# Where the residual's statistics, the weight checks and the token splits stand in a transformer block on one core

## The chip, the core and the metric

The kernel runs on one core of a Trainium2 chip. The core has five engines, each with an instruction queue of its own that runs in order: TensorE (PE in the profile, with its weight loads as PEld), VectorE (DVE), ScalarE (ACT), GpSimd (POOL) and SyncE (SP), which here issues nearly all DMAs. The metric is the device time of one execution in microseconds, as the median of three runs.

## The reference, cut to what matters

One transformer block on two sequences of 1024 tokens of 1024 numbers. Six vectors per sequence (shift, scale and gate, for attention and for the FFN) come from a conditioning vector. Then:

```python
h   = layernorm(x) * (1 + scale_a) + shift_a
q, k, v = split(clip(h @ Wqkv.T, -8, 8));  q, k = layer_norm(q), layer_norm(k)
p   = softmax(q @ k.T * 32**-0.5 + alibi, causal)          # 32 heads of 32
x1  = x + gate_a * ((p @ v) @ Wout.T)                      # the residual
h2  = layernorm(x1) * (1 + scale_f) + shift_f
g   = (h2 @ Wg.T) * ag;  u = (h2 @ Wu.T) * au              # Wg, Wu: 2752 x 1024
out = x1 + gate_f * (((silu(g) * u) @ Wd.T) * ad)
```

All data are float32. The FFN weights hold only -1, 0 and 1.

## The kernel before, in words

**Products.** Each large product is cut into two by two blocks and done with seven block products instead of eight (`SEVEN`, L780): P1, P2, U2, P5, U3, P53, U6 in this order, each a chain of matmuls into one of two PSUM banks, x and y in turn, so that a chain can begin when the bank's previous result has been read. `seven` (L843) runs such a group of chains: after every few matmuls it yields and calls `between`, and after each chain `read` evicts the bank. The sums of blocks that the scheme needs of its operands (S1 to S4, T1 to T4) are made on VectorE and GpSimd. Matmuls are recorded on L748, transposes on L751.

**Stages.** From 0 to about 580 us: modulation and the QKV projections. Then attention, with the dense work of the projections and of `output` dealt into its gaps by a planner (`together`). `output(b, js)` is the out-projection: for each sequence b it goes over pairs j of token tiles (a pair is 2 x 128 rows, four pairs a sequence). All pairs of sequence 0 and pairs 0 and 1 of sequence 1 run inside attention; pairs 2 and 3 of sequence 1 run `alone` after it (from about 1307 us), with `after=first_tokens`, so that the first FFN step is dealt in among the last pair. Then the FFN: `gate_up(b)` goes over eleven steps p of 256 of the 2752 columns, first for b=0, then b=1 (the boundary lies near 1680 us), and at the end the down product.

**One pair of `output`.** `read` copies P1, U2 and P5 on ScalarE (L1357). For P2, U3 and P53 VectorE adds the bank to the copy (L1365), GpSimd multiplies by the gate (L1366) and adds to the rows `xr` of x (L1367). For U6, VectorE multiplies the bank by the gate (L1363) and GpSimd adds it (L1367). Then `normalize` takes the statistics of the two row tiles: four `bn_stats` of 512 columns (L714) and two `bn_aggr` (L715) on VectorE, the moment the pair's chains have been issued. Each L714 waits for its L1367. The remainder is deferred: `todo.first(go)` keeps a function that the next `todo.place()` runs, inside the next pair's chains; it issues the two stores of x1 (L1380, SP) and `rest_` (L719 to L731: VectorE's small operations, ScalarE's L721 and L726, and the normalized rows, L731, over `xr`). Behind it, from chain number q0 = 3 of the next pair on, come four groups of transposes (L751), whose evictions write `h2t` (L871 on VectorE; in the last pairs half on ScalarE, L873), and `token_operands` (L1231 and L1232 on VectorE, L1233 and L1234 on GpSimd, stores to `hs` in memory on SP, L1237). An order without a semaphore between two instructions of one engine is written with `behind(a, b)`; `hold` puts an instruction behind the latest read of a bank in this way.

**One FFN step.** Two chains at a time, g and u, four banks gx, ux, gy, uy. Seven token operands hs_0 to hs_6 (1 MB each) are loaded (L1609, SP) once per sequence and split into a high and a low part: `tokens_split`, a cast on ScalarE (L1614) and a subtraction on VectorE (L1615). The weights of the next step are staged by SP (L1593), and from them `weight_operands` makes three casts on ScalarE (L1692, L1693, L1700) and four sums on GpSimd (S1 L1694, S2 L1697, S3 L1698, S4 L1699). `check_weights` counts weights that are not small integers: for each of two halves a cast to int8 on ScalarE (L1655) and a compare on VectorE (L1656). Evictions are L1808 on ScalarE, L1813 and L1828 on VectorE; silu is L1825; sums of the activations are L1769. The very first S1 has an order behind the last L1367 of sequence 1's pair 2 (`last_sum`), with no semaphore. `in_range` (L1408 to L1411) is a test of the softmax sums, four VectorE operations, issued at the end of attention.

## Time and profile before

| what | value |
|---|---|
| median of 3 runs | 2265.51 us (2263.86 to 2270.93) |
| the profiled execution | 2262.51 us, of it a span of 2260.7 us |
| TensorE busy | 2143.8 us, 95% |
| VectorE, GpSimd, ScalarE busy | 1352.1, 1098.0, 943.3 us |
| granted TensorE clock, mean | 0.984 |

Times in the profile are microseconds from the span's start. A line of a timeline gives start, duration, engine, line, operation, what it writes and reads, how many were run together, and in brackets how long the engine stood idle just before and what ended that. A line of the waits gives the sum of such idle times, their number and the longest. The lines of a table by stretch give the stretch, its length, each engine's busy time with its instructions, the granted clock, the share of the DMA engines and GB/s. Line numbers are those of the kernel before.

### The profile page before, as it was taken

To read this page: it belongs to the slowest core of one execution; us is meant where nothing else is said; L and a number is where in the kernel's file an instruction comes from. 1 tells how busy PE (TensorE), PEld (TensorE's weight loads), DVE (VectorE), ACT (ScalarE), POOL (GpSimd) and SP (SyncE) were. 2 spreads that over 40 slices of the span, in tenths; PEclk is the share of its full clock that TensorE was granted. 3 is DMA by queue.
4 is the path that set the end of the run, shared out by engine and by line. 5 is a ranking of instruction groups with operands and counts; after the bars stand their busy time and mean duration, and the time that the engine had idled before them with its cause. 6 is when DMAs were issued, how large, how long until landed. Compare 5 with 4: busy or idle time off the path is not lost. (4 is left out here: it accounts for less than half of the span.)

```text
span 2260.7 us, 27238 instructions
## 1 busy us (share of the span) xinstructions
PE 2143.8 (95%) x9537; PEld 1170.8 (52%) x9537; DVE 1352.1 (60%) x1811; ACT 943.3 (42%) x1782; POOL 1098.0 (49%) x775
## 2 busy tenths in 40 slices
PE   5999999999999999899999888899998999999998
PEld 2444444333333333232222235788877888788887
DVE  5775653455566633457667676788976555534535
ACT  1222223445444445466555414554554444333331
POOL 2330112443344554586677563677977667312212
PEclk9999999999999999999999999999999999999999
DMA  9877776545425531854553366767758777598765
GB/s 370 321 288 265 293 276 240 184 145 194 168 80 199 174 116 48 281 171 140 148 168 103 100 204 205 216 206 245 251 195 256 242 228 233 202 379 314 275 225 189
DMA packets 319349, 482.44 MB, mean 213 GB/s; under 512 B 16092, under 2 KB 235036, under 8 KB 310244
## 3 DMA queue, kind: packets, MB, share of 16 engines
q1 hardware_dynamic: 316752, 472.19, 62.4%
q10 hardware_dynamic: 2452, 8.43, 1.0%
q8 instruction: 77, 1.26, 0.2%
q14 instruction: 68, 0.56, 0.1%
HBM read 323.01 MB, written 157.55 MB: 213 GB/s over the span
## 5 line engine op out<-in xcount | busy, mean ns | idle before, releaser
L1103 ACT ACTIVATE p<-sc,kw 128x128 f32<-128x128 f32 (+3 forms) x1024 | 422.1, 513 | 390.1 <-PE sc L748 365.5
L748 PE MATMUL bank<-wT,a 128*128 128x512 f32 x768 | 366.6, 611 | 14.1 <-DVE wT L834 7.9
L1135 POOL TENSOR_TENSOR p<-p,p 128x1024 f32<-128x1024 f32 (+3 forms) x128 | 263.4, 2058 | 212.8 <-PE av L748 186.0
L1135 DVE TENSOR_TENSOR p<-p,p 128x1024 f32<-128x1024 f32 (+3 forms) x192 | 242.7, 1281 | 110.8 <-POOL p L1107 68.2
L748 PE MATMUL bank<-wB,a 128*128 128x512 f32 x576 | 270.2, 605 | 1.2 <-DVE raw L993 0.6
L748 PEld LDWEIGHTS bank<-wT,a 128*128 128x128 f32 x768 | 136.8, 191 | 200.2 <-issue 167.1
L1107 POOL TENSOR_SCALAR_AFFINE_SELECT p<-p 128x256 f32<-128x256 f32 x256 | 137.1, 548 | 182.3 <-ACT p L1103 171.3
L748 PE MATMUL sc<-cq,ck 32*128 32x512 f32 (+3 forms) x1536 | 181.6, 538 | 11.7 <-DMA ck<-qk 8.4
L748 PE MATMUL av<-p,cv 128*32 128x512 f32 (+3 forms) x1536 | 168.8, 500 | 13.2 <-POOL p L1107 13.0
L748 PEld LDWEIGHTS bank<-wB,a 128*128 128x128 f32 x576 | 102.1, 189 | 141.9 <-issue 128.8
L1899 DVE TENSOR_TENSOR lo<-lo,hi 128x1408 fp32r<-128x1408 f32 x56 | 96.3, 1723 | 93.1 <-ACT hi L1898 93.1
L748 PEld LDWEIGHTS sc<-cq,ck 32*128 32x128 f32 x1536 | 61.8, 184 | 149.8 <-issue 82.4
L1898 ACT CAST hi<-lo 128x1408 fp32r<-128x1408 f32 x56 | 76.9, 1375 | 134.0 <-DMA lo<-act 89.7
L1963 POOL TENSOR_TENSOR early_P<-early_P,x1in 128x512 f32<-128x512 f32 x16 | 35.7, 2234 | 165.1 <-DVE early_P L1961 160.3
L748 PEld LDWEIGHTS av<-p,cv 128*32 128x32 f32 x1536 | 33.7, 108 | 146.5 <-issue 80.9
L1694 POOL TENSOR_TENSOR wS<-wst,wst 128x1024 fp32r<-128x1024 f32 (+1 forms) x22 | 65.9, 2997 | 87.5 <-PE uy L748 61.9
L993 DVE TENSOR_TENSOR raw<-P,bank 128x512 f32<-128x512 f32 x48 | 32.8, 684 | 119.1 <-PE bank L748 98.9
L748 PE MATMUL gx<-hs,wS 128*128 128x512 f32 (+1 forms) x352 | 90.6, 399 | 10.6 <-ACT gP L1808 7.0
L748 PE MATMUL gy<-hs,wS 128*128 128x512 f32 (+1 forms) x352 | 89.4, 396 | 9.5 <-DVE gP L1813 6.4
L748 PE MATMUL gx<-hs,wA 128*128 128x512 f32 (+1 forms) x352 | 89.0, 393 | 1.5 <-ACT h2t L873 1.5
L748 PE MATMUL uy<-hs,wS 128*128 128x512 f32 (+1 forms) x352 | 87.2, 390 | 1.2 <-DVE uP L1813 1.2
L748 PE MATMUL ux<-hs,wS 128*128 128x512 f32 (+1 forms) x352 | 88.3, 393 | 0.0
(266 smaller groups left out, 3996.3 us busy)
## 6 DMA issues: line engine op xcount, KB each, us to landing
lo<-act SPq DMA_DIRECT2D x56, 704.0 KB
a<-hop SPq DMA_DIRECT2D x20, 1792.0 KB
wm<-in_L_wmod_dram SPq DMA_DIRECT2D x48, 512.0 KB
act<-aS SPq DMA_DIRECT2D x88, 256.0 KB
wB<-in_L_attn_Wqkv_dram SPq DMA_DIRECT2D x21, 1024.0 KB
wst<-in_L_ffn_Wg_dram SPq DMA_DIRECT2D x40, 512.0 KB
wst<-in_L_ffn_Wu_dram SPq DMA_DIRECT2D x40, 512.0 KB
qk<-qs SPq DMA_DIRECT2D x16, 1024.0 KB
```

What stands on the lines that cost most here:

```text
L748: return in_order(nc.tensor.matmul(*args, **kw_))
L993: nc.vector.tensor_add(dst, part_t[MATE[q]], bank)
L1103: last_exp[0] = nc.scalar.activation(p[:, g, lo:hi], sp[:, g, lo:hi], AF.Exp, bias=kw[:, d, h_ : h_ + 1])
L1107: last_mask[0] = nc.gpsimd.affine_select(out=p[:, :, 0:P], in_=p[:, :, 0:P], pattern=[[0, 2], [1, P]], compare_op=ALU.is_ge, fill=0.0, bas ...
L1135: adders[b](half, jb).tensor_add(dst, dst, ps[half][:, :, 0:n])
L1694: ins = nc.gpsimd.tensor_add(f["S1"], raw["A21"], raw["A22"])
L1898: nc.scalar.copy(hi, lo.bitcast(FP))
L1899: nc.vector.tensor_sub(lo, lo.bitcast(FP), hi.bitcast(FP))
L1963: eng.tensor_add(y, y, x1_of.pop(s))
```

## The change

1. `normalize` is split into `stats` and `rest_`. `output` no longer issues the statistics at the end of a pair, but hands `(stats, go)` to `todo.first`; the first `place()` runs `stats`, each `bn_stats` ordered behind the latest eviction (`last_evict`), and the next one runs `go`. For the two pairs that run alone the places begin one chain later (`when=2`), and their transposes at chain 5 instead of 3. After the very last pair both run at once.
2. `last_sum` is now the last normalized row write (L731) of sequence 1's pair 2, and the first S1 waits for it with a semaphore.
3. `in_range` moves from the end of attention to step 2 of the first `gate_up`, held behind the latest bank read.
4. The check of weight pair 1 moves from chains 4 and 5 of step 0 to chains 0 and 1 of step 1; that of pair 0 from the start of step 1 of the second sequence to chains 4 and 5 of its step 0. The token splits of the second sequence move: hs_0, 1, 2 at chains 2, 4, 6 of the last step of the first sequence and hs_3 to hs_6 at chains 0 to 3 of the next step, where there were five and two.

```diff
@@ -682,12 +682,11 @@
 
         tc.keep_in_program_order(nc.scalar.preload_act_table_set("natural_log_exp_and_others"))
 
-    def behind(ins, first):
-
+    def behind(ins, first, sync=False):
+
+        cls = mybir.DependencyClass.Sync if sync else mybir.DependencyClass.NoSync
         tc.add_manual_dep(
-            ins.ins, first.ins.name,
-            mybir.DependencyInfo(mybir.DependencyClass.NoSync, mybir.DependencyReason.DATA),
-            reason="behind",
+            ins.ins, first.ins.name, mybir.DependencyInfo(cls, mybir.DependencyReason.DATA), reason="behind",
         )
 
     last_exp = [None]
@@ -701,18 +700,28 @@
             behind(ins, last_mask[0])
         return ins
 
-    def normalize(tiles, outs, small, nm):
+    last_evict = [None]
+    last_norm = [None]
+
+    def normalize(tiles, outs, small, nm, split=False):
 
 
 
 
         n = len(tiles)
         mv = small.tile([P, n, 2], FP, tag="mv", name=f"mv_{nm}")
-        for m, t in enumerate(tiles):
-            st = small.tile([P, 2, 6], FP, tag=f"st{m}", name=f"st_{nm}_{m}")
-            for j in range(2):
-                nc.vector.bn_stats(st[:, j, :], t[:, ts(j, HALF)])
-            nc.vector.bn_aggr(mv[:, m, :], st)
+
+        def stats():
+            for m, t in enumerate(tiles):
+                st = small.tile([P, 2, 6], FP, tag=f"st{m}", name=f"st_{nm}_{m}")
+                for j in range(2):
+                    ins = nc.vector.bn_stats(st[:, j, :], t[:, ts(j, HALF)])
+                    if split and last_evict[0] is not None:
+                        behind(ins, last_evict[0])
+                nc.vector.bn_aggr(mv[:, m, :], st)
+
+        if not split:
+            stats()
 
         def rest_():
             ve = small.tile([P, n], FP, tag="ve", name=f"ve_{nm}")
@@ -728,9 +737,11 @@
             nc.vector.tensor_mul(ve, ve, rstd)
             nc.vector.scalar_tensor_tensor(rstd, ve, 1.5, rstd, ALU.add, ALU.mult)
             for m, (t, o) in enumerate(zip(tiles, outs)):
-                nc.vector.tensor_scalar(o, t, mv[:, m, 0:1], rstd[:, m : m + 1], ALU.subtract, ALU.mult)
-
-        return rest_
+                ins = nc.vector.tensor_scalar(o, t, mv[:, m, 0:1], rstd[:, m : m + 1], ALU.subtract, ALU.mult)
+            if split:
+                last_norm[0] = ins
+
+        return (stats, rest_) if split else rest_
 
 
 
@@ -868,7 +879,7 @@
         for j in range(4):
             k = 4 * g + j
             if j % 2 == 0 or not shared:
-                nc.vector.tensor_scalar(dst(k), tp[:, j, :], mul(k), add(k), ALU.mult, ALU.add)
+                last_evict[0] = nc.vector.tensor_scalar(dst(k), tp[:, j, :], mul(k), add(k), ALU.mult, ALU.add)
             else:
                 last_act[0] = nc.scalar.activation(
                     dst(k), tp[:, j, :], AF.Identity, scale=mul(k), bias=add(k)
@@ -895,27 +906,32 @@
 
         def place(self):
             if self.due is not None:
-                self.due()
-                self.due = None
+                due, self.due = self.due, None
+                if isinstance(due, tuple):
+                    due[0]()
+                    self.due = due[1:] if len(due) > 2 else due[1]
+                else:
+                    due()
 
         def add(self, go):
             self.list.append(go)
 
         def run(self, n, all_=False):
-            self.place()
+            while self.due is not None:
+                self.place()
             for _ in range(min(n, len(self.list))):
                 if not all_ and (self.banks.reserved or not self.banks.fresh()):
                     return
                 self.list.pop(0)(self.banks.turn())
                 yield TURN
 
-        def places(self, q0, n, side=lambda e: None):
+        def places(self, q0, n, side=lambda e: None, when=1):
 
             order = [q for _, _, _, q in SEVEN]
 
             def between(q):
                 side(order.index(q))
-                if order.index(q) > 0:
+                if order.index(q) >= when:
                     self.place()
                 if order.index(q) >= q0:
                     yield from self.run(n)
@@ -1360,27 +1376,30 @@
 
                 yg = part_t[MATE.get(q, "P5")]
                 if q == "U6":
-                    nc.vector.tensor_mul(yg, ga[:, ts(n, HALF)], bank)
+                    last_evict[0] = nc.vector.tensor_mul(yg, ga[:, ts(n, HALF)], bank)
                 else:
-                    nc.vector.tensor_add(yg, yg, bank)
+                    last_evict[0] = nc.vector.tensor_add(yg, yg, bank)
                     masked(nc.gpsimd.tensor_mul(yg, yg, ga[:, ts(n, HALF)]))
-                ins = masked(nc.gpsimd.tensor_add(xs[m][:, ts(n, HALF)], xs[m][:, ts(n, HALF)], yg))
-                if (b, j) == (B - 1, NJ - 2):
-                    last_sum[0] = ins
-
-            yield from seven(lambda q, i: a[q][:, i, :], bt, banks, read, todo.places(q0, 1, ahead), 2 if after else 1)
+                masked(nc.gpsimd.tensor_add(xs[m][:, ts(n, HALF)], xs[m][:, ts(n, HALF)], yg))
+
+            yield from seven(lambda q, i: a[q][:, i, :], bt, banks, read, todo.places(5 if after else q0, 1, ahead, when=2 if after else 1), 2 if after else 1)
             yield from todo.run(len(todo.list), True)
             if after is not None and j == NJ - 1:
                 after()
             xn = xs
-            rest = normalize(xs, xn, sm, f"f{b}_{j}")
-
-            def go(xs=xs, qts=qts, rest=rest):
+            stats, rest = normalize(xs, xn, sm, f"f{b}_{j}", split=True)
+
+            def go(xs=xs, qts=qts, rest=rest, j=j):
                 for m in range(2):
                     nc.sync.dma_start(x1_dram[b * NT + qts[m]], xs[m])
                 rest()
-
-            todo.first(go, b == 1 and j == NJ - 1)
+                if (b, j) == (B - 1, NJ - 2):
+                    last_sum[0] = last_norm[0]
+
+            todo.first((stats, go), False)
+            if b == 1 and j == NJ - 1:
+                todo.place()
+                todo.place()
             h2 = keep(b, j)
             for m in range(2):
                 for g in range(2):
@@ -1405,8 +1424,8 @@
 
     def in_range():
 
-        nc.vector.tensor_scalar(most, most, RS_MAX, None, ALU.is_le)
-        nc.vector.tensor_scalar(least_r, least_r, RS_MIN, None, ALU.is_ge)
+        hold(nc.vector.tensor_scalar(most, most, RS_MAX, None, ALU.is_le))
+        hold(nc.vector.tensor_scalar(least_r, least_r, RS_MIN, None, ALU.is_ge))
         nc.vector.tensor_mul(most, most, least_r)
         nc.vector.tensor_reduce(fine, most, mybir.AxisListType.X, ALU.min)
 
@@ -1568,7 +1587,6 @@
     beside[0] = False
     att.close()
     opools, _, bt, todo, _ = out_args
-    in_range()
     ff = ctx.enter_context(ExitStack())
     gu = ctx.enter_context(ExitStack())
     ffp = [ff.enter_context(tc.tile_pool(name="ff_a", bufs=1, space=PSUM))]
@@ -1693,7 +1711,7 @@
                 hold(nc.scalar.copy(f["A12"], raw["A12"]), last_copy)
                 ins = nc.gpsimd.tensor_add(f["S1"], raw["A21"], raw["A22"])
                 if (b, p) == (0, 0):
-                    behind(ins, last_sum[0])
+                    behind(ins, last_sum[0], sync=True)
                 nc.gpsimd.tensor_sub(f["S2"], g["S1"], raw["A11"])
                 nc.gpsimd.tensor_sub(f["S3"], raw["A11"], raw["A21"])
                 nc.gpsimd.tensor_sub(f["S4"], raw["A12"], g["S2"])
@@ -1740,15 +1758,16 @@
 
             def gate_up(b):
                 tiles = [hs_tiles[b, i] for i in range(7)]
+                here = None
                 for p in range(NPR):
                     n = PAIRS[p][1]
                     if p == 1:
                         pinned[0] = True
+                    if (b, p) == (0, 2):
+                        in_range()
                     if (b, p) == (0, 0):
                         operands_of[b, p] = weight_operands(p, staged.pop(0), b)
                     W = operands_of.pop((b, p))
-                    if (b, p) == (1, 1):
-                        check_weights(0, first_staged[0])
                     if p + 1 < NPR or b + 1 < B:
                         base[0] = 0 if (b, p) == (0, 0) else 2 - base[0]
                         staged.append(stage((p + 1) % NPR))
@@ -1771,19 +1790,26 @@
                             keep_act(q, act[q])
 
                     for e, (c_, qa, qb_, q) in enumerate(SEVEN):
-                        split = {(0, 0): (0, e + 2), (0, NPR - 1): (1, e - 2), (1, 0): (1, e + 5)}.get((b, p))
-                        if split is not None and 0 <= split[1] < 7:
-                            tokens_split(*split)
+                        split = {
+                            (0, 0): {i: i + 2 for i in range(5)}, (0, NPR - 1): {2: 0, 4: 1, 6: 2},
+                            (1, 0): {i: i + 3 for i in range(4)},
+                        }.get((b, p), {}).get(e)
+                        if split is not None:
+                            tokens_split(b if p == 0 else b + 1, split)
+                        if (b, p) == (0, 1) and e < 2:
+                            check_weights(1, here, (e,))
+                        if (b, p) == (1, 0) and e in (4, 5):
+                            check_weights(0, first_staged[0], (e - 4,))
                         if e == 3 and wdst is not None:
                             down_parts(p_, wdst)
                         if e == 4 and nb < B:
                             here = staged.pop(0)
                             operands_of[nb, np_] = weight_operands(np_, here, nb)
-                            if nb == 0:
+                            if nb == 0 and np_ > 1:
                                 check_weights(np_, here, (0,))
                             elif np_ == 0:
                                 first_staged[0] = here
-                        if e == 5 and nb == 0:
+                        if e == 5 and nb == 0 and np_ > 1:
                             check_weights(np_, here, (1,))
                         if b and p == NPR - 1 and e == 2:
                             for i in range(2):
```

## The prediction, as recorded before the changed kernel ran

> **What bounds the kernel now.** I read the page first, then the list of waits (all engines, then TensorE's own), then TensorE's timeline around each wait that the diff touches, then VectorE's timeline just before it, and last the busy time and clock by stretch. The page:
>
> ```profile
> span 2260.7 us, 27238 instructions
> PE 2143.8 (95%) x9537; PEld 1170.8 (52%) x9537; DVE 1352.1 (60%) x1811; ACT 943.3 (42%) x1782; POOL 1098.0 (49%) x775
> ```
>
> TensorE is the bound: 117 us of the span are all it stands idle, and no other engine passes 60%. A change that moves no matmul can only win back idle time, and the time that TensorE then runs at half clock. So the question is which idle pieces end at an instruction that the change moves.
>
> ```profile
> engine line waited for: us in total, times, longest us
> DVE st_f L714 <- POOL xr L1367: 67.9, 28, 4.8
> ```
>
> ```profile
> PE bank L748 <- DVE oP L1365: 12.0, 3, 6.4
> PE bank L751 <- DVE h2t L871: 11.2, 9, 3.8
> PE gx L748 <- ACT gP L1808: 7.0, 2, 4.6
> PE gy L748 <- DVE gP L1813: 6.4, 1, 6.4
> ```
>
> The first fence (all engines) says that VectorE, whose queue runs in order, stood 67.9 us in front of the statistics L714, because these wait for GpSimd's residual sum L1367. The second (TensorE's waits) shows who was standing behind it: bank evictions L1365 and L871. TensorE's timeline, in three places, with idle time in brackets:
>
> ```profile
> 1087.19 1.12 PE L751 MATMUL bank<-ident,xr 128*128 128x128 f32 x4 [2.21 <-DVE h2t L871]
> ...
> 1232.55 0.65 PE L751 MATMUL bank<-ident,xr 128*128 128x128 f32 x4 [3.80 <-DVE h2t L871]
> ...
> 1325.69 3.68 PE L748 MATMUL bank<-wT_o,aoS 128*128 128x512 f32 x4 [3.26 <-DVE oP L1365]
> ...
> 1360.80 3.78 PE L748 MATMUL bank<-wT_o,aoS 128*128 128x512 f32 x4 [6.36 <-DVE oP L1365]
> ...
> 1455.50 3.65 PE L748 MATMUL gx<-hs,wS 128*128 128x512 f32 x8 [4.63 <-ACT gP L1808]
> ...
> 1728.89 3.52 PE L748 MATMUL gy<-hs,wS 128*128 128x512 f32 x8 [6.42 <-DVE gP L1813]
> ```
>
> VectorE just before three of them:
>
> ```profile
> 1230.54 0.69 DVE L714 BATCH_NORM_STATS2 st_f<-xr 128x6 f32<-128x512 f32 x1 [3.06 <-POOL xr L1367]
> ...
> 1351.44 0.69 DVE L714 BATCH_NORM_STATS2 st_f<-xr 128x6 f32<-128x512 f32 x1 [1.38 <-POOL xr L1367]
> 1353.85 2.31 DVE L727 TENSOR_TENSOR ve_f<-ve_f,rstd_f 128x2 f32<-128x2 f32 x1
> 1358.62 1.53 DVE L731 TENSOR_SCALAR xr<-xr,mv_f,rstd_f 128x1024 f32<-128x1024 f32 x2
> 1360.07 0.68 DVE L1365 TENSOR_TENSOR oP<-oP,bank 128x512 f32<-128x512 f32 x1
> ...
> 1724.89 3.34 DVE L1656 SCALAR_TENSOR_TENSOR junk<-junk,wst 128x2048 int8<-128x2048 int8 x1
> ```
>
> The statistics hold VectorE, the eviction comes behind them, and TensorE waits for its bank. At 1353.85 a 128x2 operation took 2.31 us; at 1322.82 the same line took 0.16. GpSimd's first weight sums (L1694, L1697, L1699, 1351.37 to 1358.57) ran beside the slow one. At 1724.89 a check stands where an eviction is due. Last, the clock (the last-but-two column) by stretch:
>
> ```profile
> 1084.00:1092.00 8.00, 5.79 (x24) 1.74 (x24) 6.84 (x14) 3.02 (x8) 6.90 (x5) 0.79 0.48 114
> 1228.00:1240.00 12.00, 8.20 (x36) 2.56 (x38) 5.88 (x12) 4.46 (x8) 6.87 (x7) 0.86 0.40 112
> 1340.00:1370.00 30.00, 23.64 (x57) 11.03 (x56) 19.11 (x22) 4.97 (x8) 19.25 (x12) 0.83 0.39 124
> 1452.00:1462.00 10.00, 6.50 (x22) 5.31 (x23) 8.83 (x11) 4.76 (x8) 7.12 (x5) 0.83 0.54 170
> 1720.00:1735.00 15.00, 8.58 (x31) 6.61 (x31) 13.48 (x11) 4.77 (x7) 12.27 (x6) 0.77 1.00 315
> ```
>
> After each such wait TensorE gets half clock for a while: 8 x 0.21, 12 x 0.14 and 10 x 0.17 are each 1.7 us lost. The wait at 1360.80 loses 3.0: half clock runs to 1366.7 by the lengths of the matmuls, 5.9 us at half. That at 1325.69 loses 1.7, that at 1728.89 about 1.6 (half clock to 1732.0).
>
> [...]
>
> **The change, part by part.** The sum is made against the profiled execution (span 2260.7, 1.8 us around it, 2262.51 in all), which lies 3.0 under the median of 2265.51. Instructions stay the same in number on every engine but for one more table load on ScalarE.
>
> A. *Statistics a step later, while attention still runs.* Four L714 of 0.69 and two L715 of 0.2 per pair, 3.2 us of VectorE, are as long as before, but stand behind the U6 eviction of their pair or the next chain's first read, and the two stores and the rest one place later. What they waited for is then done. Gone: 2.21 + 3.80 + 0.48 (a small one at 1069.42) idle, 2 x 1.7 clock, 9.9 in all. What is late next is the rest (L719 to L731, about 2.8 us) in front of some later read: the wait at 1060.48 (2.35, L1365 behind L731) stays. The 5.66 us at 1293.36 ends at GpSimd's L1107 and stays. I take 9, bounds 4 (a wait as at 1232.55 with its clock loss, 5.5, comes up in another place) and 10.
>
> B. *The two last pairs, and the first FFN step* (1310 to 1417.9). With the statistics behind the next P2 read, L1365 at 1324.96 and 1360.07 need not wait for them. Gone: 3.26 + 1.7 + 6.36 + 3.0 = 14.3. The first weight sum now waits, by a semaphore, for L731 of pair 2; behind it on GpSimd stand L1697 and L1699 and the last pair's residual sums. By walking the new order with the old durations, L731 ends near 1350, the three sums (7.04 us) near 1357, and TensorE asks for them past 1362: hidden, with about 5 us in hand; without that cover every microsecond is one on TensorE. Pair 3 starts 8 us sooner by the walk (1336 for 1343.98), so the store of x behind which SP holds the loads of hs also goes 8 us sooner. SP now has four hs loads ahead of the h2t stores of pair 2, and x_10, x_11 behind the rb and aoA loads (which no longer wait for L1367 at 1321.28). Transposes come three chains later (q0 3 to 5), squeezed into P53 and U6, the cost of which is already in the rows (0.6 each). The four range operations (3.1 us of VectorE at 1310 to 1315) leave for a place where VectorE has slack. In the first FFN step TensorE waits eight times now, 0.93, 0.99, 1.96, 0.62, 1.60, 0.51, 0.58 and 1.48, 8.7 in all, mostly for splits of hs (L1614, L1615). These don't go with certainty, since TensorE arrives sooner and a load of 1 MB came 5.5 us after its issue (1351.87 to 1357.38). Best: 14.3 plus two thirds of 8.7, 20. Worst: 9 of the 14.3 is handed on to these waits, 5. I take 14, the eviction waits alone.
>
> C. *Checks of weight pair 1, one step later.* Two L1656 (2.28 each, 4.28 and 4.48 beside GpSimd's sums at 1441 and 1448) and two L1655 of 1.9 move from the end of the first step to chains 1 and 2 of the next. The built order puts both in front of the eviction L1813 of uy, whose bank TensorE wants 12.7 us into the step. They wait for ScalarE's copies, and these for hs stores that landed 9.4 us into it: that is a new wait of 0.5 to 5 us. Against it, the weights of the next pair (which landed at 1438.2) and their checks come sooner, and the 4.63 + 1.7 at 1455.50 shrink. I take +2, bounds -5 and 6.
>
> D. *Batch boundary.* Seven splits are dealt 3 and 4 over two steps for 5 and 2, and pair 0's two checks come out of the step where they held L1813 from 1722.68 to 1728.15. Gone there: 6.42 + 1.6. In the first step of the second batch L1614 no longer stands before L1808: 2.35, and some of 1.19 + 0.4 and 1.6 of clock. 13.5 at best; at worst the four splits (2.3 to 3.3 each), with the checks, now overrun that step, where VectorE had 11 us idle, and 2 is left. I take 8.
>
> Sum 9 + 14 + 2 + 8 = 33; 2262.5 - 33 = 2229.5 for an execution like the profiled one, 2232.5 beside the median.
>
> **The rivals.** *Handed on.* TensorE comes to the first FFN step early and stands there for hs: B is 5 and C -3, total 19, 2246.5. For it: eight waits there already, on four engines. Against it: the loads go earlier too, and DMA was at 0.39 from 1340 to 1370.
>
> *Slower: the loads of hs block the evictions.* In the new order ScalarE has L1614 of hs_0 ahead of the last pair's P5 copy, and of hs_2, hs_1 and hs_3 between the h2t evictions; VectorE has L1615 between the same. If hs_0 lands after 1351 by the walk (P5's copy must be out by 1353.4, after a cast of 1.90), TensorE waits for each load in turn. Price: seven times cast and subtraction, 1.90 + 2.28, with 1.7 of clock, 41 us, less the 5.1 that splits cost now, 36 lost, and B not gained: 9 + 8 - 36 = -19, 2284.5. The walk puts the landing at 1349, 2 us before the point.
>
> *Nothing to measure.* The new places are an order only, and all four parts come out at their low ends: 4 + 5 - 5 + 2 = 6, 2259.5. Against it: the built order does move every statistic that TensorE waited for.
>
> **How the numbers follow.** Forecast 0.66 (its own range 2217 to 2243), handed on 0.22, nothing to measure 0.06, slower 0.06. The upper bounds sum to 49, thus 2217 below; above I go to 2258, through the handed-on case with its unknowns. A difference of 0.3%, 6.8 us, is about what a measurement of this kernel can tell from none: faster 0.88, same 0.06, slower 0.06.
>
> **What would show it.** A right: no idle over 1 us before L751 near 1087 and 1233. B right: no wait for L1365 over 1 us after 1310, and the second FFN step begins by 1404 (1417.89 now). C: the waits at the second step's uy and at the third step's gx add up to less than 5. D: no wait for L1813 over 2 us in the second batch. Wrong: the L714 line of the waits still near 68, or TensorE's idle after 1310 moved to gx and gy behind L1614 or L1615.

## The result, and the profile after

| what | before | after |
|---|---|---|
| median, runs side by side | 2264.69 us (4 runs, 2259.39 to 2270.93) | 2235.15 us (4 runs, 2232.28 to 2239.52) |
| the profiled execution | 2262.51 us, span 2260.7 | 2235.17 us, span 2233.4 |
| granted clock, mean | 0.984 | 0.988 |

The ratio is 0.9879, with an interval of 0.9864 to 0.9894: the changed kernel is 1.2% faster, and 2.7 us from the forecast of 2232.5. That nearness is partly luck: profiled execution against profiled execution the gain is 27.3 us for the 33 forecast, and the stages show errors on both sides. I cut both profiled executions at the same instructions: the first matmul on the ones (end of attention), the first gx matmul of FFN step 1 (the second step; they count from 0), the starts of steps 2 and 3, and the two steps at the batch boundary.

| part | stretch | before, us | after, us | gain | forecast (bounds) |
|---|---|---|---|---|---|
| A | start to the ones | 1293.99 | 1288.06 | 5.9 | 9 (4 to 10) |
| B | ones to FFN step 1 | 123.90 | 107.12 | 16.8 | 14 (5 to 20) |
| C | FFN steps 1 and 2 | 25.56 + 31.86 | 32.48 + 32.09 | -7.2 | +2 (-5 to 6) |
| D | boundary, two steps | 31.50 + 33.54 | 27.20 + 25.39 | 12.4 | 8 (2 to 13) |
| | everything else | | | -0.7 | 0 |
| | sum | | | 27.3 | 33 |

Three parts are inside their bounds; C is outside and has the other sign. The page of the changed kernel:

```profile
span 2233.4 us, 27234 instructions
PE 2135.3 (96%) x9537; PEld 1169.8 (52%) x9537; DVE 1339.3 (60%) x1811; ACT 945.7 (42%) x1783; POOL 1100.6 (49%) x775
```

TensorE's matmuls are as many as before and 8.5 us shorter in sum (2143.8 before), at a mean granted clock of 0.988 for 0.984: half clock avoided; TensorE's idle time (the span less its busy time) is down from 117 to 98 us. The waits of all engines, then TensorE's own (sum, times, longest):

```profile
engine line waited for: us in total, times, longest us
DVE st_f L718 <- POOL xr L1383: 5.4, 4, 3.6
```

```profile
PE av L759 <- POOL p L1123: 16.4, 11, 4.8
PE uy L759 <- DVE uP L1839: 5.8, 2, 4.4
PE bank L762 <- DVE h2t L882: 4.4, 7, 1.8
PE gy L759 <- DVE gP L1839: 3.7, 1, 3.7
PE bank L759 <- DVE oP L1381: 1.2, 1, 1.2
```

The 67.9 us in which VectorE stood in front of the statistics are 5.4. Behind them the waits for the eviction oP (L1365 before, L1381 now) fell from 12.0 to 1.2, and those for h2t from 11.2 to 4.4. uy's waits rose from 1.2 to 5.8, with one of 4.4. gy's single wait for this eviction was 6.4 at the batch boundary before; it is now 3.7 and in another place. Both end at VectorE's eviction in the FFN (L1839). TensorE's timeline of the changed kernel at the places that decide:

```profile
1098.36 1.20 PE L759 MATMUL av<-p,cv 128*32 128x384 f32 x8 [2.67 <-POOL p L1123]
...
1338.44 7.03 PE L759 MATMUL bank<-wT_o,aoS 128*128 128x512 f32 x16
...
1390.39 3.35 PE L759 MATMUL gx<-hs,wA 128*128 128x512 f32 x7 [2.26 <-DVE hs L1633]
...
1412.47 3.78 PE L759 MATMUL uy<-hs,wS 128*128 128x512 f32 x8 [4.41 <-DVE uP L1839]
...
1442.44 3.78 PE L759 MATMUL gy<-hs,wS 128*128 128x512 f32 x8 [3.68 <-DVE gP L1839]
```

At 1338.44 sixteen matmuls of the last pair run without a gap, its U2 and P5, where the kernel before had 6.36 us of idle time between these two chains (1360.80). At 1412.47 and 1442.44 are the two new waits. VectorE of the changed kernel in front of each:

```profile
1400.59 1.82 DVE L1788 TENSOR_TENSOR aS<-uU,uP 128x512 f32<-128x512 f32 x1 [4.34 <-issue]
1402.44 2.79 DVE L1788 TENSOR_TENSOR aS<-aS,uP 128x512 f32<-128x512 f32 x1
...
1405.76 2.79 DVE L1674 SCALAR_TENSOR_TENSOR junk<-junk,wst 128x2048 int8<-128x2048 int8 x1
...
1408.48 3.34 DVE L1674 SCALAR_TENSOR_TENSOR junk<-junk,wst 128x2048 int8<-128x2048 int8 x1
...
1411.74 0.68 DVE L1839 TENSOR_TENSOR uP<-uP,uy 128x512 f32<-128x512 f32 x1
...
1435.84 1.32 DVE L1427 TENSOR_SCALAR most<-most 128x128 f32<-128x128 f32 x1
1437.08 1.79 DVE L1788 TENSOR_TENSOR aS<-aS,uP 128x512 f32<-128x512 f32 x1
1438.79 1.28 DVE L1428 TENSOR_SCALAR least_r<-least_r 128x128 f32<-128x128 f32 x1
1440.10 1.37 DVE L1429 TENSOR_TENSOR most<-most,least_r 128x128 f32<-128x128 f32 x1
...
1441.71 0.68 DVE L1839 TENSOR_TENSOR gP<-gP,gy 128x512 f32<-128x512 f32 x1
```

In the first group the two compares of pair 1 (L1674) stand ahead of uy's eviction, in the second the range test (L1427 to L1429, L1430 is 0.29 us more) stands ahead of gy's. From 1400.59 and from 1435.84 on VectorE runs without a pause until the eviction, which waits its turn in the queue; ahead of 1400.59 it had stood idle for 4.34 us. In the kernel before, uy's eviction of this step came ahead of the same two compares:

```profile
1429.78 0.68 DVE L1813 TENSOR_TENSOR uP<-uP,uy 128x512 f32<-128x512 f32 x1
...
1431.72 2.28 DVE L1656 SCALAR_TENSOR_TENSOR junk<-junk,wst 128x2048 int8<-128x2048 int8 x1
```

And the clock (last column but two) in three stretches of the changed kernel:

```profile
1084.00:1092.00 8.00, 7.63 (x44) 2.33 (x42) 8.00 (x13) 5.33 (x16) 6.91 (x5) 1.00 0.47 128
...
1412.00:1420.00 8.00, 7.53 (x23) 5.99 (x24) 1.86 (x3) 3.71 (x4) 2.41 (x1) 0.66 1.07 349
...
1440.00:1450.00 10.00, 7.56 (x21) 6.01 (x22) 5.97 (x8) 5.00 (x7) 3.42 (x3) 0.66 0.76 257
```

The wait near 1087 is gone and the clock there is full. After uy's wait 8 x 0.34 = 2.7 us are lost on top of the 4.41.

### The profile page after: what moved, and what is told of

It is laid out like the page before. It is cut to its first block, busy times and chain, and to the rows that moved or that the text cites. A ratio compares the mean times of both kernels' runs of the same rounds, so it can differ in the third digit from the quotient of the medians.

```text
span 2233.4 us, 27234 instructions
## 1 busy us (share of the span) xinstructions
PE 2135.3 (96%) x9537; PEld 1169.8 (52%) x9537; DVE 1339.3 (60%) x1811; ACT 945.7 (42%) x1783; POOL 1100.6 (49%) x775
## 5 line engine op out<-in xcount | busy, mean ns | idle before, releaser
L759 PE MATMUL bank<-wT,a 128*128 128x512 f32 x768 | 365.6, 610 | 14.2 <-ACT P L1000 7.6
L1123 POOL TENSOR_SCALAR_AFFINE_SELECT p<-p 128x256 f32<-128x256 f32 x256 | 135.5, 542 | 183.3 <-ACT p L1119 172.5
L1712 POOL TENSOR_TENSOR wS<-wst,wst 128x1024 fp32r<-128x1024 f32 (+1 forms) x22 | 64.1, 2915 | 92.9 <-PE uy L759 64.0
L759 PE MATMUL ux<-hs,wA 128*128 128x512 f32 (+1 forms) x352 | 87.8, 391 | 0.0
```

The lines of the kernel that those rows point to most:

```text
L759: return in_order(nc.tensor.matmul(*args, **kw_))
L1123: last_mask[0] = nc.gpsimd.affine_select(out=p[:, :, 0:P], in_=p[:, :, 0:P], pattern=[[0, 2], [1, P]], compare_op=ALU.is_ge, fill=0.0, bas ...
L1712: ins = nc.gpsimd.tensor_add(f["S1"], raw["A21"], raw["A22"])
```

## The experiments

All edits are against the changed kernel unless said. Two theories of C stood against each other from the start: that each new wait is due to the *place* where its VectorE work was put, so that another place makes it vanish, and that VectorE is *full* there, so that the work comes back as a wait elsewhere. The compare has a price of 2.28 us in some rows and 4.3 to 4.5 in others, so the second was not far-fetched. Neither theory asks when the work *arrives*, and the traces below show that this decides some of the waits.

**c_back: the check of pair 1 back where it was.**

```diff
-                        if (b, p) == (0, 1) and e < 2:
-                            check_weights(1, here, (e,))
...
-                            if nb == 0 and np_ > 1:
+                            if nb == 0:
...
-                        if e == 5 and nb == 0 and np_ > 1:
+                        if e == 5 and nb == 0:
```

> The changed kernel with the check of weight pair 1 put back to chains 4 and 5 of step 0. In the changed kernel step 1 takes 32.5 us (25.6 before the change), 4.41 us of it idle at the uy matmul, because VectorE runs both compares of pair 1 in front of the eviction of uy. Theory A (the order of VectorE's queue around that eviction is the cause, and it comes from the earlier parts of the change, not from this move): the built order of VectorE is the same in this kernel at that place, so step 1 stays at 31 to 34 us and the time at 2233 to 2238. Rival B (the move of the check is the cause): step 1 falls back to 26 us and the time to about 2228.

Measured: 2240.07 us, ratio 0.9902 (0.9881 to 0.9923). The order of VectorE around uy did not change: the compares still stand ahead of the eviction (2.79 and 3.34 us), and TensorE waits 4.29 there. Steps 1 and 2 took 32.60 and 32.23. The total lies above the 2233 to 2238 expected. The move of this check, which my prediction blamed for a uy wait in advance, is not its cause.

**c_late: the same check two chains later.**

```diff
-                        if (b, p) == (0, 1) and e < 2:
-                            check_weights(1, here, (e,))
+                        if (b, p) == (0, 1) and e in (2, 3):
+                            check_weights(1, here, (e - 2,))
```

> The changed kernel with the check of weight pair 1 at chains 2 and 3 of step 1 instead of 0 and 1, so that the eviction of uy stands in front of both compares. Theory A (order): the wait of 4.41 us at uy and its 2.5 us at half clock go, step 1 takes 25.5 to 27.5 us; up to 2 us come back in step 2; time 2228 to 2231. Rival C (load: VectorE has too much to do in steps 1 and 2, whatever the order): the wait moves to the next eviction, steps 1 and 2 together stay at 63 to 65 us, time 2234 to 2237.

Measured: 2236.85 us, ratio 0.9896 (0.9878 to 0.9914). uy's wait is gone and step 1 took 26.81, but step 2 took 36.37. TensorE's timeline of this kernel in step 2, and VectorE before it:

```profile
1436.51 3.39 PE L759 MATMUL gx<-hs,wS 128*128 128x512 f32 x8 [6.65 <-ACT gP L1834]
...
1444.16 2.11 PE L759 MATMUL gy<-hs,wS 128*128 128x512 f32 x8 [2.43 <-DVE gP L1839]
```

```profile
1422.12 4.29 DVE L1674 SCALAR_TENSOR_TENSOR junk<-junk,wst 128x2048 int8<-128x2048 int8 x1 [5.99 <-ACT junk L1673]
...
1426.35 2.87 DVE L1854 SCALAR_TENSOR_TENSOR uP<-uP,vt,gP 128x512 f32<-128x512 f32 x1
1429.14 4.44 DVE L1674 SCALAR_TENSOR_TENSOR junk<-junk,wst 128x2048 int8<-128x2048 int8 x1
...
1433.52 0.68 DVE L1839 TENSOR_TENSOR gU<-gU,gy 128x512 f32<-128x512 f32 x1
```

ScalarE's copy L1834 is named, but ScalarE itself had stood 9.13 us in front of silu (L1851, at 1434.22), until VectorE's eviction of gU at 1433.52 came out from behind two compares, with a product L1854 between them that took 2.87 instead of 0.75. These are not the compares that this edit moves: pair 1's ran at 1408.25 and 1412.29, and TensorE waited for neither. They are pair 2's, whose check the change and this run leave in its place. Nor was VectorE full: it had stood idle for 5.99 us until ScalarE's cast, and ScalarE had waited until 1419.24 for the weights of pair 2 to land. The kernel before has a wait of this kind at 1455.50 (4.63 us), with 3.67 us of idle time on VectorE ahead of pair 2's first compare at 1441.09. In the changed kernel TensorE stands at uy before that, and these two compares (1421.27 and 1427.36) cost it nothing. So 5.7 us won in step 1 were given back as 4.3 in step 2, by another wait than the one that the edit removed.

**range_late: the range test at step 6.**

```diff
-                    if (b, p) == (0, 2):
+                    if (b, p) == (0, 6):
```

> The changed kernel with the range test of the softmax sums (four VectorE operations, 1.32, 1.28, 1.37 and 0.29 us) at step 6 of the first half of the FFN instead of step 2, where they stand in front of the eviction of gy and TensorE waits 3.68 us. Theory A (order): that wait and its 2.8 us at half clock go, step 2 takes 25.5 to 26.5 us instead of 32.1, and step 6 loses nothing; time 2228 to 2230. Rival C (load): steps 1 to 6 together lose as much as now, time 2233 to 2237.

Measured: 2234.05 us, ratio 0.9875 (0.9853 to 0.9896). Step 2 took 25.39 for 32.09, with no wait of a microsecond or more, and step 6 26.62, where a step without a wait takes 25.4. So the four operations cost 6.7 us in step 2 (3.68 idle, the rest half clock) and 1.2 in step 6. The total hardly shows it: in the profiled execution the stretch from the ones to step 1 was 2.6 us longer than in the changed kernel's, and the interval is nearly 10 us wide: the 2228 to 2230 expected did not come.

**both_late: the edits of c_late and range_late together.**

```diff
-                    if (b, p) == (0, 2):
+                    if (b, p) == (0, 6):
...
-                        if (b, p) == (0, 1) and e < 2:
...
+                        if (b, p) == (0, 1) and e in (2, 3):
...
```

> Both edits of the two kernels before together: check of weight pair 1 at chains 2 and 3 of step 1, range test at step 6. Theory A (order): both gains add, 6.9 and 6.5 us, less up to 3 for compares that now end later; time 2221 to 2225. Rival C (load): at most half of it, 2229 to 2235.

Measured: 2234.95 us, ratio 0.9892 (0.9872 to 0.9911). Step 1 took 25.43 and step 2 34.47, together 59.9 for 64.6, with 6.86 us in front of gx behind L1834 (at 1437.33) and none in front of gy. The range test's wait is gone. The other is again behind pair 2's compares (1422.93 and 1429.97), and VectorE had stood idle for 6.18 us ahead of the first.

**best: the range test at step 6, and the checks of pairs 1 and 2 in the second sequence.**

```diff
-                    if (b, p) == (0, 2):
+                    if (b, p) == (0, 6):
...
-                        if (b, p) == (0, 1) and e < 2:
-                            check_weights(1, here, (e,))
+                        if b == 1 and p in (1, 2) and e in (2, 3):
+                            check_weights(p, here, (e - 2,))
...
-                            if nb == 0 and np_ > 1:
+                            if nb == 0 and np_ > 2:
...
```

> The changed kernel with the range test at step 6, and with the checks of weight pairs 1 and 2 taken out of the crowded steps 1 of the first half and done in steps 1 and 2 of the second half of the FFN (chains 2 and 3), where the same weights are staged again. Theory C (load: the wait at uy is VectorE's work of steps 1 and 2, so the compares must leave these steps, not change places within them): steps 1 and 2 of the first half take 25.4 to 27 us each (32.5 and 32.1 in the changed kernel), those of the second half 25.4 to 26.5; time 2221 to 2226. Theory A (order alone): as the kernel with both edits, steps 1 and 2 together 59 to 61 us, 2231 to 2236.

Measured: 2231.96 us (2230.52 to 2236.07), ratio 0.9858 (0.9841 to 0.9876). Steps 1 and 2 took 26.81 and 25.38, together 12.4 less than in the changed kernel. But steps 2 and 3 of the second sequence took 58.0 for 50.8: 7.2 came back. TensorE, ScalarE and VectorE of this kernel there:

```profile
1740.02 3.78 PE L759 MATMUL ux<-hs,wA 128*128 128x512 f32 x8 [4.97 <-DVE uP L1839]
```

```profile
1734.97 1.90 ACT L1673 CAST junk<-wdst 128x2048 int8<-128x2048 f32 x1 [7.18 <-DMA wdst<-in_L_ffn_Wd_dram]
```

```profile
1736.90 2.45 DVE L1674 SCALAR_TENSOR_TENSOR junk<-junk,wdst 128x2048 int8<-128x2048 int8 x1 [8.11 <-ACT junk L1673]
...
1739.28 0.68 DVE L1839 TENSOR_TENSOR uP<-uP,ux 128x512 f32<-128x512 f32 x1
```

The compare ahead of ux's eviction is that of the down weights (wdst), which this run does not move. TensorE waited for none of the four moved ones (2.40, 2.29, 2.64 and 2.29 us): step 1 of the second sequence, with two of them, took 25.48. The down weights had landed late, and VectorE stood idle for 8.11 us until ScalarE could cast them. SP had issued their load 15.7 us into the step (1727.05), in the changed kernel 4.0 (1720.58). It issued it behind a load of the next weights at 1725.96, just after the last moved cast had ended (1723.96 + 1.90). That this cast held a staging buffer, and so the loads, fits these times; no run tests it. This kernel has the lowest median of all here, yet its runs and those of the changed kernel overlap, and the 2221 to 2226 expected did not come.

**best2: pair 1 as in c_late, pair 2 in the second sequence at chains 4 and 5.**

```diff
-                    if (b, p) == (0, 2):
+                    if (b, p) == (0, 6):
...
-                        if (b, p) == (0, 1) and e < 2:
-                            check_weights(1, here, (e,))
+                        if (b, p) == (0, 1) and e in (2, 3):
+                            check_weights(1, here, (e - 2,))
...
-                            if nb == 0 and np_ > 1:
+                            if (nb == 0 and np_ > 2) or (nb, np_) == (1, 2):
...
```

> The changed kernel with the range test at step 6, the check of weight pair 1 at chains 2 and 3 of step 1, and the check of weight pair 2 not in the first half but at the usual chains 4 and 5 of step 1 of the second half, where the same weights are staged again. Theory C (load in steps 1 and 2 of the first half): these take 25.4 to 27.5 us each (32.5 and 32.1 in the changed kernel), step 1 of the second half stays under 27, since its compares stand where every other step has them and no load waits for them; with 106 to 111 us from the matmul with ones to step 1, time 2222 to 2229. Rival (the compares cost TensorE the same wherever they stand): 2231 or more.

Measured: 2234.10 us (5 runs, 2229.05 to 2241.33), ratio 0.9877 (0.9859 to 0.9894). Steps 1 and 2 took 26.85 and 25.38, so neither wait is left there. The price turned up behind pair 2's check in its new place: step 2 of the second sequence took 33.42. Its TensorE, and VectorE before it:

```profile
1716.70 3.75 PE L759 MATMUL gx<-hs,wS 128*128 128x512 f32 x8 [5.79 <-ACT gP L1834]
```

```profile
1702.30 4.29 DVE L1674 SCALAR_TENSOR_TENSOR junk<-junk,wst 128x2048 int8<-128x2048 int8 x1 [5.12 <-ACT junk L1673]
...
1709.31 4.46 DVE L1674 SCALAR_TENSOR_TENSOR junk<-junk,wst 128x2048 int8<-128x2048 int8 x1
```

The compares took nearly twice 2.28 here too, and as in c_late VectorE stood idle ahead of the first, 5.12 us, since ScalarE had waited 5.07 us, until 1699.42, for the weights. The long duration alone is not what costs: in each of steps 3 to 8 of the changed kernel two such compares run, the second taking 4.48, and these steps take 25.4 to 25.8 us. VectorE of the changed kernel in step 3:

```profile
1478.77 2.79 DVE L1674 SCALAR_TENSOR_TENSOR junk<-junk,wst 128x2048 int8<-128x2048 int8 x1
...
1481.49 2.87 DVE L1854 SCALAR_TENSOR_TENSOR uP<-uP,vt,gP 128x512 f32<-128x512 f32 x1
1484.28 4.48 DVE L1674 SCALAR_TENSOR_TENSOR junk<-junk,wst 128x2048 int8<-128x2048 int8 x1
...
1488.69 0.68 DVE L1839 TENSOR_TENSOR gU<-gU,gy 128x512 f32<-128x512 f32 x1
```

They begin 19.0 us into the step there, 26.5 in c_late and 24.2 in best2. So these waits come where a compare starts late, because its weights do, ahead of an eviction that is due; no run brings the weights sooner to test that. That VectorE is full in steps 1 and 2, the second theory, is not what the rows show; place alone, the first, does not cover it either.

**d_undo: the splits and the check of pair 0 as in the kernel before.**

```diff
+                    if (b, p) == (1, 1):
+                        check_weights(0, first_staged[0])
...
-                        split = {
-                            (0, 0): {i: i + 2 for i in range(5)}, (0, NPR - 1): {2: 0, 4: 1, 6: 2},
-                            (1, 0): {i: i + 3 for i in range(4)},
-                        }.get((b, p), {}).get(e)
+                        split = {(0, 0): (0, e + 2), (0, NPR - 1): (1, e - 2), (1, 0): (1, e + 5)}.get((b, p))
...
-                        if (b, p) == (1, 0) and e in (4, 5):
-                            check_weights(0, first_staged[0], (e - 4,))
```

> The changed kernel with the batch boundary as before: token splits five and two, the check of weight pair 0 at the start of step 1 of the second half. Theory (the dealing itself is what won the time at the boundary): the last step of the first half and steps 0 and 1 of the second take 26.3, 31.5 and 33.5 us again (26.2, 27.2 and 25.4 in the changed kernel), time 2246 to 2249. Rival (another arrival time of the loads won it): they stay near 79 us together, time 2234 to 2237.

Measured: 2248.15 us, ratio 0.9937 (0.9916 to 0.9959). The two boundary steps took 31.47 and 33.71 (27.20 and 25.39 in the changed kernel), 12.6 more, and the wait of the kernel before is back in its place, behind the second compare of pair 0 (1707.25, 3.33 us):

```profile
1711.25 3.62 PE L759 MATMUL gy<-hs,wS 128*128 128x512 f32 x8 [6.47 <-DVE gP L1836]
```

Part D is the dealing itself, splits and check taken back together here, and nothing that the earlier parts bring with them; the total, 13.0 above the changed kernel's median, agrees.

**inter: the kernel before, with later statistics for the pairs inside attention only.** Against the kernel before:

```diff
...
+            if after is None:
+                stats, rest = normalize(xs, xn, sm, f"f{b}_{j}", split=True)
+            else:
+                stats, rest = None, normalize(xs, xn, sm, f"f{b}_{j}")
...
-            todo.first(go, b == 1 and j == NJ - 1)
+            todo.first((stats, go) if stats else go, b == 1 and j == NJ - 1)
```

> The kernel before with the later statistics for the pairs inside attention alone; the last two pairs, the first weight sums, the range test, checks and splits as before. Theory: TensorE's waits near 1087 and 1233 go, attention ends (the matmul with ones that follows the longest wait near 1293) 2 to 6 us sooner, the rest takes what it took before (123.9 us from there to step 1); time 2256 to 2260. Rival (the idle time moves to the waits for the probabilities, GpSimd being later with its masks): attention ends within 1 us of before, time 2261 to 2264.

Measured: 2259.30 us (10 runs), ratio 0.9991 (0.9975 to 1.0007). The ones came at 1287.16 (1293.99 before): part A is there. From there to step 1 it took 123.06 (123.90), and both old waits for the eviction stand: 4.25 and 6.36. From the wait near 1060 to the ones it took 227.73 (233.51 in the kernel before), so part A wins about 6 us there. The total, with an interval from 5.7 us faster to 1.6 slower, does not show it.

**stats_only: the kernel before, with later statistics for all pairs, and the old order of weight sums, range test, checks and splits.** Against the kernel before it is item 1 of the change alone; against the changed kernel, in its first part:

```diff
-                if (b, j) == (B - 1, NJ - 2):
-                    last_sum[0] = last_norm[0]
...
+                if (b, j) == (B - 1, NJ - 2):
+                    last_sum[0] = ins
...
+    in_range()
...
-                    behind(ins, last_sum[0], sync=True)
+                    behind(ins, last_sum[0])
```

> The kernel before with the later statistics and transposes for all pairs, the last two included; the first weight sums ordered as before (no semaphore), range test, checks and splits as before. Theory: the out-projection's waits of 3.26 and 6.36 go by the place of the statistics alone; from the matmul with ones to step 1 it takes 106 to 112 us (123.9 before, 107.1 in the changed kernel), the boundary loses what it lost before; time 2243 to 2249. Rival (the semaphore is needed, since the first weight sums beside the small VectorE operations slow them): 114 us or more there, time 2251 or more.

Measured: 2245.84 us, ratio 0.9915 (0.9895 to 0.9936), so 17.1 us of the change come from its first item, by the medians (2262.90 for the kernel before beside it). Ones to step 1 took 109.37. Step 1 took 32.60 with 4.27 us of idle time at uy, although the check is where it was before; step 2 took 25.47, as no range test stands in it. The uy wait is therefore a part of what item 1 brings: in the kernel before, uy's eviction came ahead of the compares (1429.78, then 1431.72); with the later statistics the compares come first (1411.74, the eviction at 1417.72).

**b_nosync: the first weight sum behind the old instruction, without a semaphore.**

```diff
+                if (b, j) == (B - 1, NJ - 2):
+                    last_sum[0] = ins
...
-                if (b, j) == (B - 1, NJ - 2):
-                    last_sum[0] = last_norm[0]
...
-                    behind(ins, last_sum[0], sync=True)
+                    behind(ins, last_sum[0])
```

> The changed kernel with the first weight sums ordered behind the last residual sum of pair 2, without the semaphore on the normalized rows, as before. GpSimd alone is reordered: two of the three sums go in front of the last two token sums of pair 1 (L1249, L1250). Theory: the semaphore costs nothing and keeps these sums out of the way; without it the stores of the token sums, and behind them in SP's queue the load of hs_0, come 4 to 5 us later, the copy of the last pair's P5 (behind the cast of hs_0) too, and TensorE waits 2 to 5 us for it; 109 to 115 us from the matmul with ones to step 1, time 2236 to 2242. Rival (the order of these sums doesn't matter): 105 to 111 us, 2232 to 2237.

Measured: 2239.90 us, ratio 0.9889 (0.9874 to 0.9904). On GpSimd the sums L1712 and L1715 (1339.55 and 1341.97) now go ahead of the token operands L1249 and L1250 (1344.61). Their stores leave later, and SP, which keeps its order, issues the load of hs_0 at 1348.15 for 1339.67. What this does on ScalarE and TensorE of b_nosync:

```profile
1354.97 1.90 ACT L1632 CAST hs<-hs 128x2048 fp32r<-128x2048 f32 x1 [5.89 <-DMA hs<-hs]
1356.77 0.58 ACT L1373 COPY oP<-bank 128x512 f32<-128x512 f32 x1
```

```profile
1357.40 3.64 PE L759 MATMUL bank<-wB_o,aoS 128*128 128x512 f32 x4 [2.57 <-ACT oP L1373]
```

And ScalarE of the changed kernel:

```profile
1346.58 1.90 ACT L1632 CAST hs<-hs 128x2048 fp32r<-128x2048 f32 x1 [3.44 <-DMA hs<-hs]
1348.38 0.58 ACT L1373 COPY oP<-bank 128x512 f32<-128x512 f32 x1
```

The cast of hs_0 stands ahead of the copy of P5. Where hs_0 lands late, ScalarE waits for it with the copy behind, and TensorE waits for the copy. This is the mechanism of my slower rival, at one load and 2.57 us. In the changed kernel the load lands just in time. Ones to step 1 took 111.59 for 107.12; the totals are not far enough apart to show it.

**places_old: the alone pairs with the places of the others.**

```diff
-todo.places(5 if after else q0, 1, ahead, when=2 if after else 1), 2 if after else 1)
+todo.places(q0, 1, ahead), 2 if after else 1)
```

> The changed kernel with the places of the last two pairs as inside attention: statistics one chain sooner, transposes from chain 3 instead of 5. Theory: VectorE meets the statistics before GpSimd's sums are done, and the transposes come before the rows are normalized; TensorE waits for L1381 or the transposes as before the change; 112 to 120 us from the matmul with ones to step 1, time 2239 to 2247. Rival (deferring at all is what counts, not the chain): 105 to 111 us, 2232 to 2237.

Measured: 2248.49 us, ratio 0.9934 (0.9919 to 0.9949). Ones to step 1 took 120.0. TensorE of this kernel, first in the pair before the last and then in step 1:

```profile
1319.07 3.35 PE L759 MATMUL bank<-wT_o,aoS 128*128 128x512 f32 x4 [4.22 <-DVE oP L1381]
...
1422.95 2.11 PE L759 MATMUL uy<-hs,wS 128*128 128x512 f32 x8 [0.31 <-DVE uP L1839]
```

That the statistics are issued a step later is not enough: the chains at which statistics and transposes stand, moved together here, decide most of B. Of the two waits for the eviction one is back, the other is 0.41 (at 1348.41); over the whole stretch TensorE stood idle for 18.0 us, 9.4 in the changed kernel. The second line is a surprise of use for C: the compares stand ahead of uy's eviction here as well, but in this slower schedule the sums L1788 before them took 0.69 each (1.82 and 2.79 in the changed kernel), and TensorE waits 0.31. In the changed kernel three weight sums of GpSimd (L1712, L1715, L1717, 1396.98 to 1404.69) ran beside the two; in places_old none did, and GpSimd stood idle until 1414.22.

**before_again: the kernel before once more, with no edit,** since the half clock that I charged for short waits was read from a single execution.

> The kernel before once more, for a second profile of it: how far do two executions of one kernel differ by stage? If attention's end differs by as much as among the profiles with the change (1287.2 to 1292.7 us), the spread lies in the executions; from the wait near 1060 to the matmul with ones it should take 233 to 234 us, against 227.7 to 228.6 in every kernel with the later statistics.

Measured: 2264.86 us. The wait near 1087 of the first profile, and the clock around it, in this second execution:

```profile
1089.68 0.66 PE L751 MATMUL bank<-ident,xr 128*128 128x128 f32 x4 [2.21 <-DVE h2t L871]
```

```profile
1086.00:1094.00 8.00, 5.79 (x30) 1.97 (x27) 6.84 (x13) 3.69 (x11) 6.90 (x5) 1.00 0.32 86
```

The same wait, to the hundredth, and a clock of 1.00 for the 0.79 of the first profile. The stages agree to within 2 us: the ones at 1295.91 (1293.99), ones to step 1 123.62 (123.90).

## Why the prediction was right, and where it was not

**What bounds the kernel.** Right: the matmuls are the same in number, and the gain is 18.8 us of TensorE's idle time and 8.5 us of its busy time. VectorE's queue in front of L714 was the cause of the waits that I named.

**A: the mechanism right, 5.9 where I took 9.** The idle 2.21 and 3.80 are gone (0.37 is left at 1085.03), and the clock at 1228 to 1240 is 1.00. Two terms were off. A wait of 2.67 came up at 1098.36 for the mask L1123, which on GpSimd stands behind token operands and residual sums; I had put such a handed-on wait only into the lower bound. (Two small ones besides: the 2.35 at 1060.48, which I left standing, is 1.19, and the 0.48 at 1069.42, which I counted, is still 0.43.) And one of the two clock losses of 1.7 that I counted as gone need not occur, as before_again shows. Across the kernels here with later statistics, the stretch from the wait near 1060 to the ones took 227.5 to 231.9, against 233.5 and 233.9 in the two executions of before, so A is 2 to 6 us, mostly 5 to 6. The spread goes with the clock behind that new wait, which is 2.66 or 2.67 in all twelve: over 8 us from its start the clock was 1.00 in the eight kernels with 227.5 to 228.6, and 0.60 to 0.79 in the four with 229.9 to 231.9 (c_back, range_late, b_nosync, places_old).

**B: right, 16.8 where I took 14.** The two waits for the eviction are gone with their clock (14.3), and the idle pieces of the first FFN step fell from 8.7 to 6.5, of which 2.26 is a single wait for a split of hs at 1390.39. Over the whole stretch TensorE's idle time fell from 21.7 to 9.4 us and its busy time by 4.5. By stats_only (109.37) and places_old (120.0), it is the first item with its later places that does it, not the semaphore. The semaphore's part was costed at nothing, with cover to spare; b_nosync suggests that it is worth a few microseconds, but the same stretch took 105.1 to 110.7 us in kernels that do not differ in it (best2, best), so its size is open.

**C: wrong, the failed step.** I took +2, and it was -7.2, below my lower bound of -5. Two terms failed.

First, "the four range operations (3.1 us of VectorE at 1310 to 1315) leave for a place where VectorE has slack". It stands under B, and I put the cost at nothing; it fell due in C's stretch. The place had no slack: they took 4.26 us in step 2, stood ahead of gy's eviction, and cost 3.68 idle and 3.0 of clock, 6.7 by range_late. I had looked at the place that they leave and never at the queue of the place that they reach. A row was there: with 4.63 us of idle time at 1455.50, TensorE already waited behind VectorE in step 2 of the kernel before.

Second, the uy wait. I named it, at 0.5 to 5 us, and at 4.41 it is in the range, but I left out its 2.7 of half clock and gave it the wrong cause, the moved check. Moved in the program, this check hardly moved in time: in the kernel before its compares ran at 1431.72 and 1433.93, 13.8 us into step 1 already, and those at 1441 and 1448, whose prices I quoted, are pair 2's. stats_only and c_back have it with the check in its old place. What is shown is that the later statistics, with the later places of the alone pairs, change the order so that the compares come before the eviction; in places_old the same order costs only 0.31. Of the 4.1 us between the two, 2.4 are the longer operations of VectorE, by which uy's eviction starts 16.6 us into the step instead of 14.2. The other 1.7 are TensorE's own: in places_old it comes to uy that much later, since its first matmuls of the step ran at half clock (eight in 3.60 us at 1408.04, for 1.98) after a wait of 2.25. GpSimd's weight sums ran beside the sums L1788 here and not in places_old; why they fall there when step 1 begins some 13 us earlier was not isolated.

Rows bear on those durations. In the kernel before, the compares at 1431.72 and 1433.93 took 2.28 each while GpSimd stood idle, as it did for 7.09 us until 1438.34. Where GpSimd's sums ran beside it, the same compare took up to 4.49, but not each time: in the changed kernel 2.30 at 1504.15 and 4.48 at 1509.18, both beside weight sums. The 2.79 and 3.34 are between; the first ran beside GpSimd's sums L1788 throughout and the second for 1.18 us (they end at 1409.66). No run here takes away GpSimd's work beside one and the same compare, so what sets the duration there is not shown.

The part that I expected on the other side, that the 4.63 at 1455.50 with its clock would shrink, did come, but not for my reason: no such wait for gx is left in step 2, because TensorE stops at uy before it. In c_late and both_late, where it does not stop there, the wait is back with 6.65 and 6.86. And the sign that I had set for C, waits for uy and for gx of less than 5 together, was met (4.41 and none) and missed the loss, since it did not look at gy.

**D: right, 12.4 where I took 8.** Almost the best case of 13.5. The fear that four splits overrun the first step of the second sequence was idle; d_undo shows the dealing as the cause.

**The rivals.** *Handed on* was right in kind at the wrong place: B did not hand its gain to the loads of hs, but some of it returned as uy's wait in step 1. *Slower* does exist, 2.57 us in b_nosync and 2.47 in stats_only (at 1355.24), for one load in place of seven. In the changed kernel hs_0 landed at 1346.6, earlier than the 1349 of my walk, but the pair came earlier too: P5's copy behind the cast ended at 1348.96 and P53 began at 1349.01, so there was no cover to speak of where I had counted 2 us. Had the load come later, it would have cost its lateness, as b_nosync shows. *Nothing to measure* fell.

So the total was near because C's error of 9 and A's of 3 stood against 3 and 4 too little in B and D. That left 5.7 us too little between the profiled executions. Between the medians it is 2.7, because I had added 3.0 for the kernel before, whose median lay that far above its profiled execution; the changed kernel's does not. None of the five kernels that repair C in part or in whole beat the changed kernel beyond its spread: 2231.96 for best, 2234.05 for range_late, 2234.10 for best2, 2234.95 for both_late and 2236.85 for c_late against 2235.15.

## What to carry to other kernels

A moved step has two ends: cost the queue that it joins as carefully as the wait that it leaves, counting when its own input arrives, which eviction comes due just behind it, and how long it takes there (the compare here took 2.28 to 4.49 us). Before calling an engine full, look whether it stood idle just ahead: the compares that held TensorE up in c_late and best2 began after 5 to 6 us of idle VectorE, late with their weights, while compares as long cost nothing in steps 3 to 8. And read a total of 0.1 to 0.3% from the stage where it arises, since a stage of 30 us shows 5 us that a median of 2235 with its spread does not.

## What the runs showed of the hardware that I had not expected

A wait of 2.21 us was followed by half clock (0.79 over 8 us) in one execution and by full clock (1.00) in another of the same kernel, and one of 2.26 us (at 1390.39 in the changed kernel) was followed by 0.83 over 1386 to 1396. The wait of 2.67 us for the mask L1123 had either outcome too, here in the changed kernel and then in c_back (granted clock in the last column but two):

```profile
1095.66:1103.66 8.00, 5.33 (x27) 1.71 (x30) 2.04 (x3) 2.13 (x5) 7.92 (x9) 1.00 0.63 208
```

```profile
1097.27:1105.27 8.00, 5.33 (x19) 1.40 (x18) 2.05 (x3) 0.18 (x1) 7.92 (x9) 0.60 0.64 208
```

In the kernel before, the 2.35 us in front of 1060.48 were followed by a clock of 1.00 over the 8 us from there. My prediction had half clock after each such wait; the rows show that waits of 2.2 to 2.7 us were sometimes followed by it and sometimes not. No run here shows what decides it.
